# Seven block products in place of eight for a graph network's messages

## The chip, the cores and the metric

The kernel runs on one core of one Trainium2 chip. Its time is the device time of one execution in microseconds; the figure before the change is the median of three runs, 1519.66 us (1519.43 to 1519.81). One further execution was profiled; the hardware profiler gives it a span of 1517.7 us.

## The reference

Four graph layers run one after the other on 64 graphs of 256 nodes with 128 features, all in fp32. Every layer ends in a residual sum and a layer norm, x = layernorm(x + layer(x)). All layers use one weighted adjacency matrix `adj` (256x256). Layer 0 is the one that the change concerns: five steps of a gated recurrent unit whose input is the message `adj @ h`.

```python
def step(h, _):
    m_in = jnp.einsum('nm,bmd->bnd', in_matrix, h)
    m_out = jnp.einsum('nm,bmd->bnd', out_matrix, h)
    av = jnp.concatenate([m_in, m_out], axis=-1)
    u3 = h @ u3_w.T + u3_b
    z = jax.nn.sigmoid(av @ w3_w.T + w3_b + u3)
    r = jax.nn.sigmoid(av @ w4_w.T + w4_b + u3)
    hv = jnp.tanh(av @ w5_w.T + w5_b + (r * h @ u5_w.T + u5_b))
    h = (1.0 - z) * h + z * hv
    return (h, None)
...
x = _layernorm(x + _L0_gnn_ref(x, adj, adj, ...), axis=-1)
```

In and out matrix are the same here, so a step needs one message per graph. Layer 1 mixes two linear maps by a row softmax of edge values (a diagonal part and the rest), layer 2 is an attention layer followed by a graph isomorphism layer, and layer 3 is a polynomial of third order in `adj`.

## The kernel before

Graphs are worked on in pairs, so there are 32 pairs. A pair's state is one tile of 128 partitions by 512 columns. It exists in two layouts. In the layout by tokens, node t*128+p of graph b lies on partition p, in block 2b+t of four blocks of 128 features. In the transposed layout features lie on the partitions and the 512 columns are the nodes of both graphs.

`spread` (L505) forms a message: for either graph two products of 256 columns, the two node blocks of the state being the weights and the two block rows of the transposed adjacency `aT` the moving operand. The result is the transposed message of both graphs in one PSUM bank, and `to_sbuf` copies it to SBUF (`evacuate`, L210 on ACT or L211 on DVE). In terms of 128x128 blocks that is eight products for a message.

A step of layer 0 (`layer0`) then runs in the transposed layout: two products of 512 columns for the gate r (L599, L600), a tanh on ACT (L603), r*h on DVE (L605), one more product into the same bank for the gate z (L607) with a tanh (L609), two products for the candidate (L614, L615) with a tanh (L617), and three DVE operations for the new state (L619, L620, L622). The new state is turned to the layout by tokens for the next message. `turn` does this by a 32x32 block transpose on DVE (L486), one write to DRAM (L488) and four reads from it (L494), all in SP's queue; for the last pairs, as many as `BY_DMA` says for each place, TensorE transposes it instead (L480), with a copy out of PSUM.

The work of 32 pairs is interleaved, and no order is written out by hand. Every piece of work is an `Op` with the values that it reads and writes and one or more ways (an engine, an assumed duration, a function). When the program is built, `Schedule.order` plays the work through: among the operations whose inputs are there and for which a tile is free, it takes the one that can start first, ties going to the one that is latest against a due time (`DUE`, `LAST_DUE`, `LAST`, `HOLD`). The assumed durations are scaled by `MARGIN`, and a consumer on another engine sees a result `LAG` plus `SEEN` later. A way named "DVE+" or "POOL" also takes a common resource "PORT", so the plan doesn't put such operations of the two engines side by side. The instructions of each engine are issued in the order so found, and each waits for the others by semaphores. Buffers are the tiles of `CLASSES`: 34 tiles of class A (512 columns), six of class B (1024), eight PSUM banks (PS), and so on.

Of the kernel before, what the change touches and what calls it, by code (L numbers as in the profile page):

```python
# [9 lines left out]
ALU = mybir.AluOpType  # L10
AX = mybir.AxisListType

P = 128
N = 256
D = 128
STEPS = 5

BY_DMA = {"h": 1, "y": 1, "x1": 2, "x2": 1, "w": 0, "z": 1, "x3": 1}

WARM = 4  # L20

TURN, TT = 0.44, 0.61
# [12 lines left out]

CLASSES = {"X": (512, 15), "T": (512, 3), "A": (512, 34), "H": (520, 4), "B": (1024, 6), "S": (32, 64), "PS": (512, 8), "D": (512, 4), "E": (1024, 8)}

# [4 lines left out]

DUE, LAST_DUE, LAST = 15.0, 7.0, 6

MARGIN, LAG = 1.1, 0.3

HOLD = (0.0, 0.0, 0.0, 110.0)

# [24 lines left out]


class Op:
    def __init__(self, pair, ways, reads, writes, number, dma):
# [5 lines left out]
class Schedule:  # L82
# [6 lines left out]
    def add(self, ways, r=(), w=(), dma=None):  # L89

        op = Op(self.pair, ways, list(r), list(w), len(self.ops), dma)
        for v in op.reads:
            op.before.update(dict.fromkeys(v.writers))
        for v in op.writes:
            op.before.update(dict.fromkeys(v.readers))
        for v in op.reads:
            v.readers.append(op)
        for v in op.writes:  # L100
            v.writers.append(op)
        op.before.pop(op, None)
        op.layer = self.layer
        self.ops.append(op)
        return op
# [5 lines left out]
    def order(self, tiles):  # L111
        for op in self.ops:
            op.waits = len(op.before)
            for b in op.before:
                b.then.append(op)
            for v in dict.fromkeys([*op.reads, *op.writes]):
                v.left += 1
# [7 lines left out]
        while ready:  # L125
            best = None
            for op in ready:
                held = 0.0
                for v in op.writes:
                    if v.cls and v.ap is None:  # L130
                        held = max(held, min((t for t, _ in free[v.cls]), default=1e9))
                if held == 1e9:
                    continue
                for engine, us, fn in op.ways:
                    us = us if engine == "PE" else us * MARGIN
                    start = max(op.ready, held, *(engines[e] for e in USES.get(engine, (engine,))))
                    late = self.due(op.pair) - op.rest + HOLD[op.layer] if op.pair >= 0 else -1e4
                    key = (start + (us if len(op.ways) > 1 else 0.0), late, op.number)
                    if best is None or key < best[0]:
                        best = key, start, op, engine, us, fn  # L140
# [3 lines left out]
            ready.remove(op)  # L144
            for v in op.writes:
                if v.cls and v.ap is None:
                    slot = min(free[v.cls], key=lambda s: s[0])
                    free[v.cls].remove(slot)
                    v.ap = slot[1]
# [6 lines left out]
            out.append((start, op.number, op, fn))  # L156
            for v in dict.fromkeys([*op.reads, *op.writes]):
                v.left -= 1
                v.end = max(v.end, end + op.seen)
                if not v.left and v.cls:  # L160
                    free[v.cls].append((v.end, v.ap))
# [6 lines left out]

            for v in dict.fromkeys([*op.reads, *op.writes]):
                op.__dict__.setdefault("tiles", {})[v] = v.ap  # L170
        assert len(out) == len(self.ops), "operations that wait for one another"
# [5 lines left out]
def kernel(ctx: ExitStack, tc: tile.TileContext, x, xT, adj, adjT, mats, cols, rows, out):  # L177
# [8 lines left out]
    def fixed(shape, name, dtype=F32):  # L186
        return Value(ap=const.tile([P, *shape], dtype, name=name), name=name)
# [190 lines left out]
    for it in range(2):  # L378
# [4 lines left out]
        dve(0.3, lambda it=it, blk=blk: nc.vector.tensor_sub(blk(), blk(), dg.ap[:, it, :]), [lg, dg], [lg])  # L383

    drow, offT = fixed([N], "drow"), fixed([2, N], "offT")

    def diagonal():
        for it in range(2):
            nc.tensor.matmul(t4.at(2, P)[:, it, :], ones.ap[:, :P], dg.ap[:, it, :], start=True, stop=True)
    pe(mm(256), diagonal, [ones, dg], [t4])  # L390
    dve(0.4, lambda: nc.vector.tensor_copy(drow.ap, t4.at(N)), [t4], [drow])
    pe(0.45, lambda: turned(t5.at(2, N), lg.at(2, N)), [lg, ident], [t5])
# [51 lines left out]
    dve(0.25, lambda: nc.vector.tensor_add(vq.ap[:, 1, :], mat("v3"), mat("v6")), [W1], [vq])  # L444

    centre(vx, lambda: vx.ap, 2)
    centre(vq, lambda: vq.ap, 2)
# [51 lines left out]
    def spread(i, right):  # L499

        t = Value("PS", name="ps")
        for b in range(2):
            def fn(b=b):
                for j in range(2):
                    nc.tensor.matmul(t.at(2, N)[:, b, :], tokens(i)[:, 2 * b + j, :], right.ap[:, j, :],  # L505
                                     start=(j == 0), stop=(j == 1))
            pe(mm(512), fn, [i, right], [t])
        return t

    def stats(y, eps=None):  # L510
# [81 lines left out]
    def layer0(x0, hT):  # L592
        h = x0
        for s in range(STEPS):
            mT = to_sbuf(spread(h, aT), "mT")
            t = Value("PS", name="ps")
# [16 lines left out]
            def candidate(t=t, mT=mT, r=r):  # L613
# [4 lines left out]
                [t, bzrh], [hv])  # L618
            dve2(TT, lambda hv=hv, hT=hT: nc.vector.tensor_sub(hv.at(512), hv.at(512), hT.at(512)), [hv, hT], [hv])  # L619
            dve2(TT, lambda hv=hv, z=z: nc.vector.scalar_tensor_tensor(hv.at(512), z.at(512), 1.0, hv.at(512),  # L620
# [5 lines left out]
        y = Value("A", name="y")  # L626
        dve2(TT, lambda: nc.vector.tensor_add(y.at(512), h.at(512), x0.at(512)), [h, x0], [y])
        layer_norm(y, x0)
# [11 lines left out]
    def layer1(x1):  # L640
        qT = to_sbuf(spread(x1, offT), "qT")
        xb, dd = Value("A", name="xb"), lambda: drow.ap[:, None, :].to_broadcast([P, 2, N])
        if by_dma("x1"):
            dT = turn(x1, "dT", "x1")
            dve_or_pool(lambda e: e.tensor_mul(dT.at(2, N), dT.at(2, N), dd()), [drow, dT], [dT])
        else:
            t, dT = transposes(x1), Value("A", name="dT")
            dve(TT, lambda: nc.vector.tensor_mul(dT.at(2, N), t.at(2, N), dd()), [t, drow], [dT])
        dve_or_pool(lambda e: e.tensor_add(tokens(xb), tokens(x1), row("l1_bias", 4)), [x1, rbc], [xb])
# [5 lines left out]
    def layer2(x2):  # L655
# [19 lines left out]

        nm, nm2, den, d2 = (lambda k=k: s.at(32)[:, 4 * k:4 * k + 4] for k in range(4))
        d2v = Value("S", name="d2")
# [5 lines left out]
        def largest():  # L683
            nc.vector.tensor_add(nm(), nm(), hs()[:, :, D])
            nc.vector.tensor_scalar(nm2(), nm(), -1.0, None, op0=ALU.mult)
            nc.vector.scalar_tensor_tensor(nm(), nm(), -0.2, nm2(), op0=ALU.mult, op1=ALU.min)
        dve2(0.5, largest, [s, h], [s])
        for c in range(4):
# [129 lines left out]
```

## Time and profile before

| | before |
|---|---|
| time, median of 3 runs | 1519.66 us |
| profiled span | 1517.7 us |
| TensorE busy | 1509.9 us |
| DVE busy | 1183.2 us |
| ACT busy | 901.1 us |
| Pool busy | 363.0 us |
| messages, `aT` with a state (L505, 1024 records of 256 columns) | mean length 379 ns |
| DMA engines, share of the span in their main queue | 69.5% |

The busy time of an engine is the time in which at least one of its instructions was running. A product in fp32 is two matmul records in the profile, each with its own weight load (PEld). A matmul's recorded length includes the time until its result is out, and the next one starts earlier than that; the distance between starts is what a product costs in a stream. The granted TensorE clock is full in nearly the whole run.

### The profile page before, as it was taken

What the parts mean: (1) busy time and instruction counts of PE and PEld (TensorE: products, weight loads), DVE (VectorE), ACT (ScalarE), POOL (GpSimd) and SP (SyncE); (2) the same over time, 40 slices, a digit from 0 to 9 for tenths busy, and PEclk for the clock granted to TensorE, in tenths of its full rate; (3) what the DMA queues carried; (4) which work ended last, traced back from release to release, by engine and by line L of the source; (5) the groups of instructions that cost most, each with busy time, mean ns of one, the idle gap of its engine ahead of it and who ended that gap; (6) DMA issues with size and microseconds to landing.
All of it is one profiled execution on the core that took longest, in us unless ns stands there. A gap on an engine that the chain in (4) does not pass through costs nothing.

```text
span 1517.7 us, 22720 instructions
## 1 busy us (share of the span) xinstructions
PE 1509.9 (99%) x6300; PEld 1052.0 (69%) x6300; DVE 1183.2 (78%) x2774; ACT 901.1 (59%) x2497; POOL 363.0 (24%) x461
## 2 busy tenths in 40 slices
PE   9999999999999999999999999999999999999998
PEld 6555666666666767777677767666776676779987
DVE  6467878788898889888878778778787877887763
ACT  3444445566667767767556565656565556676752
POOL 0000001122323413332222303112331122224542
PEclk9999999999999999999999999999999999999999
DMA  8354557678688697888868777848777767575552
GB/s 240 71 116 92 121 115 150 139 141 164 147 174 165 141 191 147 171 153 173 168 130 174 153 153 160 160 98 164 140 148 152 148 132 146 102 146 116 122 128 64
DMA packets 949454, 216.79 MB, mean 143 GB/s; under 512 B 728144, under 2 KB 944848, under 8 KB 949328
## 3 DMA queue, kind: packets, MB, share of 16 engines
q1 hardware_dynamic: 949328, 215.34, 69.5%
q8 instruction: 51, 0.84, 0.2%
q14 instruction: 75, 0.61, 0.1%
HBM read 117.12 MB, written 98.11 MB: 142 GB/s over the span
## 4 chain that ended last, share of the span: by engine, by line
PE 99%; SPq 0%; DMA 0%; issue 0%; DVE 0%; POOLq 0%; ACT 0%; ACTq 0%; POOL 0%; DVEq 0%
PE ps L505 29%; PE ps L614 9%; PE ps L607 9%; PE ps L615 9%; PE ps L599 9%; PE ps L600 9%; PE ps L636 8%; PE ps L705 4%; PE ps L751 4%; PE ps L743 4%; PE ps L744 4%; PE ps L664 2%; SPq L494 0%; PE ps L270 0%; PE ps L480 0%; DMA a<-e 0%
## 5 line engine op out<-in xcount | busy, mean ns | idle before, releaser
L210 ACT COPY a<-ps 128x512 f32<-128x512 f32 (+1 forms) x295 | 160.3, 545 | 187.3 <-PE ps L505 129.5
L505 PE MATMUL ps<-aT,a 128*128 128x256 f32 x1024 | 242.7, 379 | 0.3 <-DMA a<-e 0.3
L505 PEld LDWEIGHTS ps<-aT,a 128*128 128x128 f32 x1024 | 193.4, 190 | 69.0 <-issue 46.1
L603 ACT ACTIVATE a<-ps,bzrh 128x512 f32<-128x512 f32 x160 | 109.9, 687 | 166.6 <-PE ps L600 160.2
L617 ACT ACTIVATE a<-ps,bzrh 128x512 f32<-128x512 f32 x160 | 109.8, 686 | 164.2 <-PE ps L615 158.6
L614 PE MATMUL ps<-a,w 128*128 128x512 f32 x320 | 163.5, 592 | 0.0
L600 PE MATMUL ps<-a,w 128*128 128x512 f32 x320 | 163.4, 592 | 0.0
L615 PE MATMUL ps<-a,u5h 128*128 128x512 f32 x320 | 163.4, 592 | 0.0
L607 PE MATMUL ps<-a,w 128*128 128x512 f32 x320 | 162.9, 592 | 0.0
L636 PEld LDWEIGHTS ps<-W,a 128*128 128x128 f32 x1024 | 128.9, 192 | 21.6 <-issue 19.1
L486 DVE STREAM_TRANSPOSE a<-a 128x512 f32<-128x512 f32 x186 | 131.0, 706 | 11.5 <-ACT a L582 4.2
L571 POOL TENSOR_TENSOR s<-s,neg_half 128x4 f32<-128x4 f32 x128 | 137.6, 1075 | 10.1
L605 DVE SCALAR_TENSOR_TENSOR a<-a,a 128x512 f32<-128x512 f32 x128 | 88.3, 690 | 62.6 <-ACT a L603 59.9
L609 ACT ACTIVATE a<-ps,bzrh 128x512 f32<-128x512 f32 x160 | 109.9, 687 | 45.4 <-PE ps L607 43.2
L619 DVE TENSOR_TENSOR a<-a,a 128x512 f32<-128x512 f32 x128 | 90.0, 703 | 54.4 <-ACT a L617 54.3
L636 PE MATMUL ps<-W,a 128*128 128x128 f32 x1024 | 131.3, 275 | 0.0
L599 PE MATMUL ps<-a,W 128*128 128x512 f32 x256 | 130.8, 593 | 0.0
L524 POOL TENSOR_SCALAR s<-s 128x4 f32<-128x4 f32 x64 | 21.5, 336 | 451.9 <-DVE s L521 443.0
L620 DVE SCALAR_TENSOR_TENSOR a<-a,a 128x512 f32<-128x512 f32 x160 | 117.3, 733 | 12.2 <-ACT a L609 7.3
L568 POOL TENSOR_SCALAR s<-s 128x4 f32<-128x4 f32 x96 | 28.5, 297 | 392.0 <-ACT a L563 306.5
L505 PE MATMUL ps<-aT,x 128*128 128x256 f32 x512 | 121.4, 380 | 0.0
L615 PEld LDWEIGHTS ps<-a,u5h 128*128 128x128 f32 x320 | 60.8, 190 | 76.5 <-issue 66.0
(181 smaller groups left out, 2730.3 us busy)
## 6 DMA issues: line engine op xcount, KB each, us to landing
e<-a SPq DMA_DIRECT2D x278, 256.0 KB
a<-e SPq DMA_DIRECT2D x1112, 64.0 KB
e<-b SPq DMA_DIRECT2D x32, 512.0 KB
b<-e SPq DMA_DIRECT2D x128, 128.0 KB
x<-x_in SPq DMA_DIRECT2D x32, 256.0 KB
t<-xT_in SPq DMA_DIRECT2D x32, 256.0 KB
a<-d SPq DMA_DIRECT2D x32, 256.0 KB
y_out<-a SPq DMA_DIRECT2D x32, 256.0 KB
```

The costliest lines, as they stand in the source:

```text
L210: S.add([("ACT", us[0], lambda: nc.scalar.copy(o(), i())), ("DVE", us[1], lambda: nc.vector.tensor_copy(o(), i()))], r, w)
L486: dve(n / 512 * 0.55 + 0.09, lambda: nc.vector.transpose(st.at(n), i.at(n)), [i], [st])
L505: nc.tensor.matmul(t.at(2, N)[:, b, :], tokens(i)[:, 2 * b + j, :], right.ap[:, j, :], start=(j == 0), stop=(j == 1))
L571: pool(1.02, lambda: nc.gpsimd.tensor_tensor(rs(), rs(), neg_half.ap, op=ALU.pow), [s, neg_half], [s])
L599: nc.tensor.matmul(t.at(512), mat("u3"), hT.at(512), start=True, stop=False)
L600: nc.tensor.matmul(t.at(512), w4.ap, mT.at(512), start=False, stop=True)
L603: act(0.59, lambda t=t, r=r: nc.scalar.activation(r.at(512), t.at(512), AF.Tanh, bias=bzrh.ap[:, 1:2], scale=0.5), [t, bzrh], [r])
L607: pe(mm(512), lambda t=t, mT=mT: nc.tensor.matmul(t.at(512), w3.ap, mT.at(512), start=False, stop=True, skip_group_check=True), [w3, mT, t ...
L614: nc.tensor.matmul(t.at(512), w5.ap, mT.at(512), start=True, stop=False)
L615: nc.tensor.matmul(t.at(512), u5h.ap, r.at(512), start=False, stop=True)
L620: dve2(TT, lambda hv=hv, z=z: nc.vector.scalar_tensor_tensor(hv.at(512), z.at(512), 1.0, hv.at(512), op0=ALU.add, op1=ALU.mult), [hv, z], ...
L636: nc.tensor.matmul(tokens(t)[:, c, :], tokens(i)[:, c, :], w(), start=(k == 0), stop=(k == len(lefts) - 1))
```

## The change

For steps 1 to 4 of layer 0 a new helper `spread7` takes the place of `spread` and `to_sbuf`. It treats the state blocks of both graphs and the blocks of `aT` as two 2x2 block matrices and forms their product from seven block products of 128 columns. The recipe needs four sums of state blocks (`add`, in DVE or Pool, chosen by the planner) and four differences of adjacency blocks (`aTt`, formed once). The products go to the four quarters of one PSUM bank, X, Y, Z and V. X, V and Z get two products each and Y one, and X, V and Z are read in between. The first product opens the whole bank. Two copies (`copy`, ACT or DVE) and three sums with a PSUM operand (`plus`, DVE) bring the message together in SBUF. `Part` is a value that stands for a part of a tile, so that the planner orders the parts one by one.

Step 0 of layer 0 and the messages of the other layers keep `spread`. With it come smaller edits. One subtraction of every step of layer 0 (L619) and the residual sum (L627) may go to Pool. Layer 1 scales its input by the diagonal ahead of the turn (on ACT, DVE or Pool), and the diagonal is kept as a column that a DVE reduction makes, no longer as a row that TensorE makes. A small maximum in layer 2 takes two DVE operations for three. The numbers of pairs that are turned by TensorE at the end, the due times, `MARGIN`, `LAG`, `HOLD` and the number of B tiles have new values.

```diff
-BY_DMA = {"h": 1, "y": 1, "x1": 2, "x2": 1, "w": 0, "z": 1, "x3": 1}
+BY_DMA = {"h": 1, "y": 2, "x1": 0, "x2": 1, "w": 3, "z": 3, "x3": 0}
...
+FAST = (1, 2, 3, 4)
...
-DUE, LAST_DUE, LAST = 15.0, 7.0, 6
-MARGIN, LAG = 1.1, 0.3
-HOLD = (0.0, 0.0, 0.0, 110.0)
+DUE, LAST_DUE, LAST = 20.0, 7.0, 12
+MARGIN, LAG = 1.03, 0.8
+HOLD = (0.0, 0.0, -20.0, 110.0)
...
-    def diagonal():
-        for it in range(2):
-            nc.tensor.matmul(t4.at(2, P)[:, it, :], ones.ap[:, :P], dg.ap[:, it, :], start=True, stop=True)
-    pe(mm(256), diagonal, [ones, dg], [t4])
-    dve(0.4, lambda: nc.vector.tensor_copy(drow.ap, t4.at(N)), [t4], [drow])
+    dve(0.3, lambda: nc.vector.tensor_reduce(dcol.ap, dg.ap, AX.X, ALU.add), [dg], [dcol])
...
+    aTt = fixed([4, P], "aTt")
+    blk_a = lambda j, i: aT.ap[:, j, i * P:(i + 1) * P]
+    for k, (p_, q_) in enumerate(((lambda: blk_a(0, 1), lambda: blk_a(0, 0)), (lambda: blk_a(1, 1), lambda: aTt.ap[:, 0, :]),
+                                  (lambda: blk_a(1, 1), lambda: blk_a(0, 1)), (lambda: blk_a(1, 0), lambda: aTt.ap[:, 1, :]))):
+        dve(0.25, lambda k=k, p_=p_, q_=q_: nc.vector.tensor_sub(aTt.ap[:, k, :], p_(), q_()), [aT, aTt], [aTt])
...
+    def spread7(h, right, terms):
...
+        def add(o, x, y, op, r, w):
+            fn = lambda e: e.tensor_tensor(o(), x(), y(), op=op)
+            S.add([("DVE+", 0.2, lambda: fn(nc.vector)), ("POOL", 0.36, lambda: fn(nc.gpsimd))], r, w)
...
+        product(0, H(0, 0), B(0, 0), [h], [X, Y, Z, V], start=True)
+        copy(lambda: blk(o, 3), 0, [X], [o3])
+        add(s1, H(1, 0), H(1, 1), ALU.add, [h], [p1])
+        add(s2, s1, H(0, 0), ALU.subtract, [h, p1], [p2])
+        add(s3, H(0, 0), H(1, 0), ALU.subtract, [h], [p3])
+        add(s4, H(0, 1), s2, ALU.subtract, [h, p2], [p4])
+        product(0, H(0, 1), B(1, 0), [h, X], [X])
+        copy(lambda: blk(o, 0), 0, [X], [o])
+        product(1, s2, T(1), [p2, Y], [Y])
+        plus(lambda: blk(sv, 1), 1, lambda: blk(o, 3), [Y, o3], [p2])
+        product(2, s1, T(0), [p1, V], [V])
+        product(3, s3, T(2), [p3, Z], [Z])
+        plus(lambda: blk(sv, 0), 2, lambda: blk(sv, 1), [V, p2], [p1])
+        product(2, s4, B(1, 1), [p4, V], [V])
+        plus(lambda: blk(o, 3), 3, lambda: blk(sv, 0), [Z, p1, o3], [o])
+        product(3, H(1, 1), T(3), [h, Z], [Z])
+        plus(lambda: o.at(4, P)[:, 1:3, :], 2, lambda: blk(sv, 1)[:, None, :].to_broadcast([P, 2, P]), [V, Z, p2], [o], 2)
+        return o
...
-            mT = to_sbuf(spread(h, aT), "mT")
+            mT = spread7(h, aT, aTt) if s in FAST else to_sbuf(spread(h, aT), "mT")
...
-            dve2(TT, lambda hv=hv, hT=hT: nc.vector.tensor_sub(hv.at(512), hv.at(512), hT.at(512)), [hv, hT], [hv])
+            dve_or_pool(lambda e, hv=hv, hT=hT: e.tensor_sub(hv.at(512), hv.at(512), hT.at(512)), [hv, hT], [hv])
...
-            dve_or_pool(lambda e: e.tensor_mul(dT.at(2, N), dT.at(2, N), dd()), [drow, dT], [dT])
...
+        S.add([("ACT", 1.26, scaled), ("DVE+", TT, lambda: nc.vector.tensor_mul(xd.at(2, 2, D), x1.at(2, 2, D), dc())),
+               ("POOL", 1.27, lambda: nc.gpsimd.tensor_mul(xd.at(2, 2, D), x1.at(2, 2, D), dc()))], [x1, dcol], [xd])
+        dT = turn(xd, "dT", "x1")
...
-            nc.vector.tensor_add(nm(), nm(), hs()[:, :, D])
-            nc.vector.tensor_scalar(nm2(), nm(), -1.0, None, op0=ALU.mult)
-            nc.vector.scalar_tensor_tensor(nm(), nm(), -0.2, nm2(), op0=ALU.mult, op1=ALU.min)
-        dve2(0.5, largest, [s, h], [s])
+            nc.vector.scalar_tensor_tensor(nm(), nm(), -1.0, hs()[:, :, D], op0=ALU.mult, op1=ALU.subtract)
+            nc.vector.scalar_tensor_tensor(nm(), nm(), 0.2, nm(), op0=ALU.mult, op1=ALU.min)
+        dve2(0.25, largest, [s, h], [s])
```

## Prediction

> **What bounds the kernel now.** I began with the page's totals, then the chain that ended last, then who waits for whom on TensorE.
>
> ```profile
> span 1517.7 us, 22720 instructions
> PE 1509.9 (99%) x6300; PEld 1052.0 (69%) x6300; DVE 1183.2 (78%) x2774; ACT 901.1 (59%) x2497; POOL 363.0 (24%) x461
> PE 99%; SPq 0%; DMA 0%; issue 0%; DVE 0%; POOLq 0%; ACT 0%; ACTq 0%; POOL 0%; DVEq 0%
> ```
>
> PE is busy 99% and the chain lies on PE for 99%. A busy PE need not be a full one, so I asked for PE's own waits:
>
> ```profile
> PE ps L270 <- DVE ones L268: 1.2, 1, 1.2
> PE ps L505 <- DMA a<-e: 0.3, 1, 0.3
> ```
>
> After the first 1.2 us PE waits 0.3 us in the whole run. The span is PE's work plus 7.8 us at both ends (1517.7 - 1509.9), so a microsecond of PE work taken away is a microsecond gained as long as PE still never waits. The price of a product comes from start-to-start distances in PE's timeline (columns: start, length, engine, line, count), since lengths overlap:
>
> ```profile
> 704.35 1.95 PE L705 MATMUL ps<-h,b 128*128 128x128 f32 x16
> 706.14 0.60 PE L743 MATMUL ps<-vx,a 128*128 128x256 f32 x2
> ...
> 713.04 1.89 PE L505 MATMUL ps<-aT,a 128*128 128x256 f32 x8
> 713.24 0.69 ACT L603 ACTIVATE a<-ps,bzrh 128x512 f32<-128x512 f32 x1 [2.23 <-PE ps L600]
> ...
> 714.76 1.02 PE L607 MATMUL ps<-a,w 128*128 128x512 f32 x2
> ```
>
> A product is two records. Eight products of 128 columns take 706.14 - 704.35 = 1.79 us, 0.2238 each; four of 256 take 714.76 - 713.04 = 1.72, 0.430 each. Half the columns cost 52%. The ACT row gives the way out of PE: L600's successor starts at 713.04, ACT reads the result at 713.24, 0.20 us later.
>
> DVE is next; where it is fullest it is busy 174.0 of 200 us:
>
> ```profile
> 400.00:600.00 200.00, 199.67 (x842) 135.16 (x841) 174.04 (x388) 140.69 (x400) 62.33 (x69) 1.00 0.83 165
> ```
>
> Two more readings are needed, a 128-column DVE sum and a meeting of DVE and Pool:
>
> ```profile
> 35.21 0.28 DVE L443 TENSOR_TENSOR vq<-W 128x128 f32<-128x128 f32 x1
> 35.42 0.28 DVE L444 TENSOR_TENSOR vq<-W 128x128 f32<-128x128 f32 x1
> ...
> 617.71 1.55 POOL L710 TENSOR_TENSOR a<-a,rbc 128x512 f32<-128x512 f32 x1 [5.66 <-ACT a L582]
> 618.17 1.11 DVE L684 TENSOR_TENSOR s<-s,h 128x4 f32<-128x4 f32 x1
> ```
>
> The sum lasts 0.28 us and gives way after 0.21. L684, four columns wide and 0.165 us at its median, took 1.11 us: it stood until Pool's product was over.
>
> **The Trainium skill.** TensorE: Matmul & The Clock Gate, Part 2, Step-by-step: the drain of one matmul overlaps the fill of the next. The trace agrees: 0.275 us long, 0.112 apart at 128 columns. SBUF - State Buffer, Who interferes with whom: a DVE instruction with two SBUF inputs contends with a GpSimd one that reads SBUF, and the later one blocks; L684 shows it. PSUM - Partial Sum Buffer, PSUM bank collisions: guard PSUM by bank, not by address. No run yet shows the collision, but the changed program's order shows the guard: a product into one quarter of a bank waits for ACT's or DVE's read of another quarter. GPSIMD Engine Reference, 3.1: about 2.6 cycles an element for two inputs. Here 512 columns take 1.28 us (median) and four 0.20, so I estimate 0.47 us for 128.
>
> **The change part by part.** The changed program's order, counted by line, does what the words say: 512 products of 256 columns (steps 1 to 4 of 32 pairs) become 896 of 128; step 0 keeps its own.
>
> PE. Per message 4 x 0.430 = 1.720 becomes 7 x 0.2238 = 1.567; 128 messages save 128 x 0.153 = 19.6 us. Twenty more 128x128 transposes stand in the last pairs (60 for 40; in PE's timeline four of them stand from 1470.61 to 1471.05, so 0.11 each): +2.2. The diagonal's two products go: -0.45. Net -17.9 us.
>
> DVE. Adds in SBUF that the order gives it: 329; sums out of PSUM: 384 of 128 and 128 of 256 columns; 53 small copies. At 0.28, 0.28, 0.415 (L666) and about 0.29 that is 268 us; by start distances (0.20, 0.20, 0.35, 0.20), 198. Off DVE go 119 wide two-input operations (0.69: -82), 32 scalings of L535 (-11), the shortened maximum of layer 2 (-6), six wide copies (-4), and transposes and others (-7): -110. DVE gets to 1271 to 1341 us. Lock waits come on top: the means of the wide rows lie above their medians by some 27 us in all with 70 wide Pool operations; with 168 and 183 small ones I estimate 65 to 80. So some 1310 to 1390 us of about 1500, 87 to 93%.
>
> Pool: 183 x 0.47 + 98 x 1.28 = +211 us, 574 in all. ACT: 203 copies of 128 columns (0.27 from the 256 and 512 rows) for 114 of 512 (0.583), and 124 more row scalings (0.39): about +40. Both stay below 65% and are hidden beside PE, apart from waits below.
>
> The buffers: a message holds one PSUM bank of eight from first product to last read, and an A tile of sums of 34; B gets a seventh tile. The order already has these limits, so their price shows as distances in it. The turn of h through DRAM has more room than before: between the candidate product and the next step's first product stand at least 14.6 us of other PE work (12.3 before, where PE never waited). The x1 scaling before the turn, the moved subtraction and sum, and the new due times sit in stretches with more than 2.6 us of slack, longer than a lock wait (1 us): nothing. SP issues the same 278 + 1112 turns, and 29 + 116 for the attention weights instead of 32 + 128; the queue is off the path before: nothing. The four differences of the adjacency (4 x 0.28) come before DVE's first wait for layer 0 while PE runs step 0: nothing. At the two ends PE is idle for 7.8 us, and 6.3 of it is the chain after the last product (its group ends at 1511.4, the span at 1517.7), which stays; another order there can give or take 1 us, and I count none.
>
> The added wait is the real cost. Within a message PE writes a bank, ACT or DVE reads it, and PE writes it again. A product that waits holds everything behind it on PE. One such exchange takes 0.20 (out of PE) + 0.28 (the sum) + 0.05 (ones written at 1.15, used at 1.20) + 0.19 (weight load) = 0.73 us; 0.55 if the weights are in place. Along the PE order I added up the work that stands between the last product a read needs and the product that waits for that read. Before, the least is 1.7 us. After, 28 places have under 1 us: eight have 0, three 0.22, two 0.43, three 0.45, two 0.67, ten 0.86. At 0.73 they lose 8 x 0.73 + 3 x 0.51 + 2 x 0.30 + 3 x 0.28 + 2 x 0.06 = 8.9 us; at 0.55, 6. Stretches where several reads stand in line add twelve places and 7.6 us (5.4 at the lower price). So 11.3 to 16.5 us of new PE waits, none of it below zero since PE had none to give back. I take 12.5: nearer the lower end, as a wait may not hold up the weights.
>
> Sum: 1517.7 - 17.9 + 12.5 = 1512.3 for the profiled span; the timed runs (1519.43 to 1519.81) stand 2.0 above it, so 1514.
>
> **Rivals.** A, the above: 1514, own range 1510 to 1516.6. For it: PE's own sum is certain. Against: the waits nearly match it.
> B, the exchanges cost little, because other engines are ahead and the weights are loaded early: at most 5 us, 1502 to 1507. For it: PE waited 0.3 us before. Against: places with no work at all between.
> C, the waits reach 16 to 20 us: 1518 to 1522, no change.
> D, slower: the lock between Pool and DVE. DVE runs at 87 to 93%, in its fullest stretches near 98; there it can't catch up a 1 us wait, and a bank's sum comes late to PE. I estimate 70 such waits; if one in five reaches PE that is 14 us on A, 1528. One in thirteen decides (5.4 us more make it 1519.7), one in eight makes it slower by 0.2%. Against: in the program before 174 of 200 busy us on DVE let PE wait 0.3.
> That the change isn't what it says is excluded by the count.
>
> **How the numbers follow.** A measurement tells 0.2%, 3 us, from no change. A 0.48, B 0.12, C 0.15, D 0.25. Faster is A + B, 0.60; same 0.15; slower 0.25. The time is A's, 1514. The range takes in most of B and D: 1503 to 1529. A's and B's own is 1502 to 1516.6.
>
> **What would show it.** PE's work near 1492 us; the 128-column product at 0.224 apart. PE waits of 11 to 17 us, nearly all before products of the new message, released by its sums and copies, 0.5 to 0.75 us each. DVE between 1310 and 1390. B is right if PE waits under 5 us; D if it waits over 24, with DVE rows of over 1 us beside Pool's. I am wrong in the base if 128-column products stand clearly further apart than 0.224.

## The result, and the profile after

The changed kernel takes 1545.24 us (median of 6 runs, 1544.45 to 1549.03), the kernel before beside it 1519.74 us. The ratio is 1.0173, 95% interval 1.0159 to 1.0186: slower, by 25.5 us. I had forecast 1514 us, faster, and a range that ended at 1529.

The page after (span; PE, DVE and the others; the chain by engine):

```profile
span 1542.4 us, 25912 instructions
PE 1507.8 (98%) x7088; PEld 1059.9 (69%) x7088; DVE 1359.0 (88%) x3465; ACT 919.0 (60%) x2725; POOL 598.2 (39%) x742
PE 32%; DVE 6%; DMA 2%; issue 1%; ACT 1%; SPq 1%; POOL 0%; POOLq 0%; ACTq 0%; DVEq 0%
```

The chain no longer lies on PE from end to end. Its shares add up to 43% only, so I read no more from it than that it leaves PE. Who waits for whom on PE, after (us in total, times, longest):

```profile
PE ps L538 <- DVE a L542: 11.9, 21, 2.0
PE ps L538 <- ACT a L545: 2.9, 6, 0.9
PE ps L538 <- DVE a L534: 2.6, 4, 0.8
PE ps L538 <- DVE a L546: 1.8, 5, 0.6
PE ps L670 <- DVE a L542: 1.6, 1, 1.6
```

L538 is a product of the new message, L542 a sum that reads its bank. Before, PE waited 0.3 us in all once it had started. Is a product itself dearer than I thought? PE's timeline, after:

```profile
703.87 0.83 PE L538 MATMUL ps<-aTt,a 128*128 128x128 f32 x6
704.53 0.39 PE L538 MATMUL ps<-aT,a 128*128 128x128 f32 x2
704.76 1.95 PE L692 MATMUL ps<-W,a 128*128 128x128 f32 x16
```

Four products of two records start within 704.76 - 703.87 = 0.89 us, 0.222 each. The price stands, so the time is lost between products. I added, over all neighbours in PE's record, what a start-to-start distance has above the plain one (0.112 us for a record of 128 columns, 0.216 for 256, 0.430 for 512), where that is over 0.04 us. I call this sum PE's gaps: 3.9 us before, 47.0 after. It is more than the waits view shows, because after a wait PE also loses some 0.16 us of overlap between records (one of 128 columns is 0.275 us long, and the next starts 0.112 after it). What is left of the spans is the work: (1542.4 - 47.0) - (1517.7 - 3.9) = -18.4 us. So the change saves what it should, and 43 us of gaps take it back and more.

One stretch and one group of DVE rows point to the reason. First the window from 400 to 600 us, columns as before:

```profile
400.00:600.00 200.00, 193.28 (x907) 133.17 (x908) 184.19 (x465) 121.63 (x359) 71.78 (x89) 1.00 0.72 145
```

DVE went from 174.0 to 184.2 busy us there. Then rows of DVE (busy us, mean ns of one). The first line is the kernel before, whose L620 is L676 after:

```profile
L620 DVE SCALAR_TENSOR_TENSOR a<-a,a 128x512 f32<-128x512 f32 x160 | 117.3, 733 | 12.2 <-ACT a L609 7.3
```

```profile
L676 DVE SCALAR_TENSOR_TENSOR a<-a,a 128x512 f32<-128x512 f32 x160 | 123.3, 774 | 3.7
L534 DVE TENSOR_TENSOR a<-a,a 128x128 f32<-128x128 f32 x194 | 72.8, 379 | 4.8
```

Both read two operands from SBUF. A sum of 128 columns, which lasts 0.285 us while Pool is idle, lasts 0.38 on average. I counted the DVE instructions that last over 0.1 us more than the median of their own row while a two-input operation of 128 columns or more runs on Pool: 46 before, 33 us of extra length in all; 168 after, 101 us. No other DVE instruction is that much longer than its row's median, in either kernel. In what follows these 46 and 168 instructions are called held, and their extra length held time.

### The profile page after: what moved, and what is told of

It reads as the page before. It is cut to its first block, busy times and chain, and to the rows that moved or that the text cites. A ratio compares the mean times of both kernels' runs of the same rounds, so it can differ in the third digit from the quotient of the medians.

```text
span 1542.4 us, 25912 instructions
## 1 busy us (share of the span) xinstructions
PE 1507.8 (98%) x7088; PEld 1059.9 (69%) x7088; DVE 1359.0 (88%) x3465; ACT 919.0 (60%) x2725; POOL 598.2 (39%) x742
## 5 line engine op out<-in xcount | busy, mean ns | idle before, releaser
L542 DVE TENSOR_TENSOR a<-ps,a 128x128 f32<-128x128 f32 (+1 forms) x512 | 156.9, 315 | 63.9 <-PE ps L538 47.0
L538 PEld LDWEIGHTS ps<-aTt,a 128*128 128x128 f32 x1024 | 150.4, 191 | 71.3 <-issue 42.7
L538 PE MATMUL ps<-aTt,a 128*128 128x128 f32 x1024 | 170.4, 277 | 11.8 <-DVE a L542 4.5
L538 PEld LDWEIGHTS ps<-aT,a 128*128 128x128 f32 x768 | 120.4, 191 | 65.2 <-issue 37.7
L496 DVE STREAM_TRANSPOSE a<-a 128x512 f32<-128x512 f32 x215 | 150.8, 704 | 6.9 <-ACT a L704 0.9
L538 PE MATMUL ps<-aT,a 128*128 128x128 f32 x768 | 139.3, 279 | 9.3 <-DVE a L542 7.4
L220 ACT COPY a<-ps 128x512 f32<-128x512 f32 (+1 forms) x173 | 90.0, 523 | 92.4 <-PE ps L515 57.4
L627 POOL TENSOR_TENSOR s<-s,neg_half 128x4 f32<-128x4 f32 x128 | 139.9, 1093 | 10.3
L692 PEld LDWEIGHTS ps<-W,a 128*128 128x128 f32 x1024 | 128.9, 192 | 18.6 <-issue 16.5
L534 POOL TENSOR_TENSOR a<-a 128x128 f32<-128x128 f32 x121 | 66.5, 563 | 188.2 <-DMA a<-e 133.2
L545 ACT COPY a<-ps 128x128 f32<-128x128 f32 x203 | 51.1, 266 | 141.6 <-DVE a L542 71.9
L676 DVE SCALAR_TENSOR_TENSOR a<-a,a 128x512 f32<-128x512 f32 x160 | 123.3, 774 | 3.7
L515 PE MATMUL ps<-aT,x 128*128 128x256 f32 x512 | 123.7, 380 | 1.4 <-DMA x<-x_in 1.4
```

Of the source, the lines that this page charges most:

```text
L496: dve(n / 512 * 0.55 + 0.09, lambda: nc.vector.transpose(st.at(n), i.at(n)), [i], [st])
L538: pe(mm(128), lambda: nc.tensor.matmul(blk(t, k), left(), rt(), start=start, stop=True, skip_group_check=True), [*r, right, terms], w)
L542: dve(0.065 + 0.135 * n, lambda: nc.vector.tensor_add(to(), t.at(4, P)[:, k:k + n, :], other()), r, w)
L627: pool(1.02, lambda: nc.gpsimd.tensor_tensor(rs(), rs(), neg_half.ap, op=ALU.pow), [s, neg_half], [s])
L692: nc.tensor.matmul(tokens(t)[:, c, :], tokens(i)[:, c, :], w(), start=(k == 0), stop=(k == len(lefts) - 1))
```

## Experiments: the numbers of the planner, and eight products

What I expected of these runs speaks of three theories of the new gaps. G: the program guards a PSUM bank as a whole, and the planner doesn't know that. L: DVE reads the bank late because Pool holds up DVE. R: seven products with reads between them need more exchanges of a bank than any order can hide.

**Old numbers.** All edits, with BY_DMA, DUE, LAST, MARGIN, LAG and HOLD of before (one line of the edit is shown).

```
-MARGIN, LAG = 1.03, 0.8
+MARGIN, LAG = 1.1, 0.3
```

> The changed kernel with the planner's numbers of before (turns, due times, margin 1.1, lag 0.3, hold). Theories G and R: a lag of 0.3 leaves less room between a read and the product behind it (by distances in the order 43 places under 1 us after another quarter's read, where the changed kernel has 25), so slower than the changed kernel, 1555 to 1580. Theory L: Pool gets as much work, DVE somewhat less, so 1535 to 1550. A theory that the new numbers are to blame: under 1525.

Measured: 1631.92 us, ratio 1.0735 (1.0719 to 1.0751); gaps 134 us, 59 of them after 1400 us. That is above all the ranges that I gave: with the old numbers the seven products do far worse, so going back to them is no cure.

**Eight products, new numbers.**

```
-FAST = (1, 2, 3, 4)
+FAST = ()
```

> All edits of the change but the seven products: no step uses them, every message keeps eight. Theories G, L and R, which all lay the loss on the new message: 1516 to 1523, PE waits under 4 us. A theory that the new numbers or the smaller edits are to blame: above 1530.

Measured: 1545.68 us, ratio 1.0168 (1.0153 to 1.0184). By the time alone one would blame the other edits and call the seven products a wash. The trace says otherwise: of 27.9 us of gaps 21.6 lie after 1400 us. The stretch from 1500 us to the end at 1544, columns as above:

```profile
1500.00:1546.00 46.00, 22.67 (x85) 17.82 (x83) 12.67 (x48) 6.47 (x17) 7.87 (x11) 0.69 0.12 29
```

PE is busy for 22.7 us of these 44, at a mean clock of 0.69: the last pairs come late and PE runs dry. With these numbers this order ends badly; that is not the changed kernel's illness, which has 1.3 us of gaps after 1400 us.

**Eight products, old numbers.** Both edits together.

> The kernel after with FAST = () and all planner numbers of the kernel before: every other edit of the change stays (diagonal by DVE, scaling before the turn, moved subtraction, 20 more turns on TensorE or fewer, 0.45 us of diagonal less). Theory T (the trace of the run with FAST = () and the new numbers has 21.6 of its 28.0 us of TensorE gaps after 1400 us, so the new numbers, and not the other edits, leave the last pairs late when the messages are of eight products): 1518 to 1525 us. Theory S (the small edits themselves cost the 26 us): 1540 us or more.

Measured: 1527.71 us, ratio 1.005 (1.0033 to 1.0067). That lies between my two ranges: the other edits alone cost 8 us, not 26, and not nothing. Gaps are 12.7 us, 6.6 of them after 1400 us; the longest is a wait of 3.5 us at L801 for a DMA. So the numbers make 18 of the 26 us of the run before, and against this kernel the seven products as they were built lose 17.5 us. I can't say which edit makes the 8.

**The bank as one value.** The planner treats the four quarters as separate values, but the program that comes out guards a bank as a whole. Here the planner knows it.

```
-        X, Y, Z, V = (Part(t) for _ in range(4))
+        X = Y = Z = V = t
```

> The planner treats the four quarters of a message's PSUM bank as one value, so that its order knows that a product waits for the read of any quarter; nothing else differs from the changed kernel. Theory G (the waits come from the guard by bank that the planner doesn't know of): PE's waits fall from 43 us to under 20, time 1515 to 1525. Theory L (the reads are late because DVE stands behind Pool's locks): about the same as the changed kernel, 1538 to 1550. Theory R (seven products with reads in between need more exchanges than any order can hide): PE still waits 35 us or more, now before products that follow a read of their own quarter, 1537 to 1555.

Measured: 1586.58 us, ratio 1.0437 (1.0416 to 1.0457), gaps 90.7 us, 21 of them after 1400 us. That is above the ranges of all three theories. A planner that knows the bank doesn't avoid the waits by that alone: it makes another order, which loses more. Why so much isn't settled.

## Experiments: what Pool holds

In the runs of this section, all but the last, the instructions of PE and DVE stand in the order of the changed kernel, so only durations differ, and what Pool does besides.

**Short Pool operations.** All two-input operations that the planner had given to Pool work on 8 columns of each block in place of all (8 to 32 columns in place of 128 or 512). One of four lines of this kind:

```
-        S.add([("DVE+", TT, lambda: fn(nc.vector)), ("POOL", 1.27, lambda: fn(nc.gpsimd))], r, w)
+        S.add([("DVE+", TT, lambda: fn(nc.vector)), ("POOL", 1.27, lambda: fn(Narrow(nc.gpsimd)))], r, w)
```

> The order of the changed kernel with every two-input operation that it gives to Pool cut to 8 columns of each block (the rest of those sums and products is left out; the A tiles are set to zero at the start), so Pool holds the shared port for a short time only. Theory L: DVE busy falls by 60 us or more and PE's waits from 43 us to under 22, time 1515 to 1525. Theory G: DVE busy falls too, but PE's waits stay above 32 us, 1534 to 1545. Theory R: as G.

Measured: 1529.45 us, ratio 1.0063 (1.0048 to 1.0078). My zeroing of the tiles at the start had put one gap of 8.7 us into it, at 19 us. The same without that:

> As the earlier kernel with short Pool operations, but without zeroing the tiles on Pool at the start (which made one wait of 8.7 us at 19 us there): the first 24 two-input operations on Pool stay whole, every later one works on 8 columns, so work is left out; the order is that of the kernel after. Theory L (Pool's hold of the port makes DVE late, and TensorE waits for DVE): 1529.45 less 8.7, so 1519 to 1523 us. Theory R (the exchanges of seven products with DVE and ACT cost the same whatever Pool does): over 1535 us.

Measured: 1517.43 us, ratio 0.9982 (0.9975 to 0.9989). The loss is gone, and a small gain shows, a little more than theory L had it. But short operations also leave Pool free sooner, and their results come sooner. The next run, the hold-free one, takes the first away: after each cut operation Pool computes a power on 4 columns (or 1), which keeps it busy about as long as the wide one did. A cut operation's own result can still be out before the power is done; but in the changed kernel all waits that end with Pool's wide operations or state sums add up to 2.9 us: 2.2 by TensorE's weight loads, 0.7 by ACT, none by a product.

```
+            f(cut(o), cut(x), cut(y), **k)
+            n = 4 if int(np.prod(o.shape[1:])) >= 256 else 1
+            self.e.tensor_tensor(Narrow.scratch[:, :n], Narrow.one[:, :n], Narrow.half[:, :n], op=ALU.pow)
```

> The order of the kernel after. Each two-input operation of Pool after the first 24 works on 8 columns (work left out) and is followed on Pool by a power on 4 columns (1.09 us by the rows of the profile, and no DVE row is longer beside it) or on 1 column for the sums of 128: Pool is about as long busy as after, but holds nothing of DVE. Theory L (it is the hold of the port that makes DVE late): 1517 to 1524 us, as with short operations. Theory Q (it is that Pool's results come late, whoever holds what): 1535 to 1547 us.

Measured: 1516.59 us, ratio 0.9976 (0.9967 to 0.9985). Its page and its PE waits (L560 and L564 are the lines of L538 and L542):

```profile
span 1515.2 us, 26245 instructions
PE 1498.8 (99%) x7088; PEld 1060.6 (70%) x7088; DVE 1267.7 (84%) x3465; ACT 920.3 (61%) x2725; POOL 634.7 (42%) x1069
```

```profile
PE ps L560 <- DVE a L564: 4.5, 11, 0.8
PE ps L560 <- ACT a L567: 2.0, 5, 0.5
```

Pool is even longer busy than after (634.7 for 598.2 us), and DVE has the same 3465 instructions in 91 us less; held time falls from 101 us to 2. So it is not Pool's load but that a two-input operation of 128 columns or more on Pool holds DVE. The record of PE has the same 7088 matmuls in both, so they can be compared one by one: at 88 places the changed kernel's gap is longer by over 0.04 us, 28.3 us in all; elsewhere shorter by 1.4. That is 26.9 of the 27.2 us between the spans; 20.0 us stand at 62 products of the new message. One of the 88, in the changed kernel:

```profile
985.70 1.27 POOL L675 TENSOR_TENSOR a<-a,a 128x512 f32<-128x512 f32 x1 [4.50 <-ACT a L673]
985.76 1.35 DVE L534 TENSOR_TENSOR a<-a,a 128x128 f32<-128x128 f32 x1
986.92 1.32 POOL L768 TENSOR_TENSOR a<-a,rbc 128x512 f32<-128x512 f32 x1
987.04 1.75 DVE L661 SCALAR_TENSOR_TENSOR a<-a,a 128x512 f32<-128x512 f32 x1
991.53 0.91 DVE L542 TENSOR_TENSOR a<-ps,a 128x128 f32<-128x128 f32 x3
992.49 0.38 PE L538 MATMUL ps<-aT,a 128*128 128x128 f32 x1 [1.96 <-DVE a L542]
```

The same instructions with Pool's cut:

```profile
963.76 0.29 DVE L556 TENSOR_TENSOR a<-a,a 128x128 f32<-128x128 f32 x1
963.97 0.68 DVE L683 SCALAR_TENSOR_TENSOR a<-a,a 128x512 f32<-128x512 f32 x1
967.39 0.90 DVE L564 TENSOR_TENSOR a<-ps,a 128x128 f32<-128x128 f32 x3
968.81 0.61 PE L560 MATMUL ps<-aT,a 128*128 128x128 f32 x4
```

Held, a sum of 0.29 us takes 1.35 and a product of 0.68 takes 1.75, 2.1 us more together. The sum ends 0.14 us after Pool's first operation, the product 0.55 us after the second, most of its own length. DVE takes its queue in order, so the sums that free the bank, behind five more instructions, start at 991.53 - 985.76 = 5.77 us after that sum instead of 967.39 - 963.76 = 3.63. Pool never appears as the releaser of PE; the waits view names DVE, and only DVE's row shows a length that isn't its usual one.

The Trainium skill, SBUF - State Buffer, Who interferes with whom: a DVE instruction with two SBUF inputs contends with a GpSimd one that reads SBUF, one with at most one SBUF input, outside the modes that use both ports, does not. The trace of the changed kernel agrees: of the adds at L534 those that lie for over half their length beside a two-input Pool operation of 512 columns take 1.01 us on average (36 of them), beside one of 128 columns 0.42 (12), those with Pool idle 0.285 (210). The sums of L542 of 128 columns, with one operand in PSUM, take 0.285 us in both cases, and the transposes of L496 0.70. Of the 168 held instructions 167 have two operands in SBUF. (A power on 4 columns is an exception to the section's rule; see the end.)

**Only the wide ones cut.** Operations of 256 and 512 columns are cut, the sums of 128 stay whole.

> The order of the kernel after. Of Pool's two-input operations after the first 24 counted, only those of 512 columns (or 256) are cut to 8 columns (work left out); the state sums of 128 columns stay whole on Pool. Theory W (the holds of 1.3 us by the wide operations, most of which before the change were there too but struck a DVE with nothing urgent, make TensorE wait): 1518 to 1526 us. Theory N (the 183 new sums of 128 columns on Pool do it, by their number): 1535 us or more.

Measured: 1522.41 us, ratio 1.0011 (1.0005 to 1.0018): 22.8 of the 28.7 us that the hold-free run takes off, inside theory W's range. The 183 new short sums on Pool stand for the other 6.

**Only those that the change moved.** Before, the subtraction (L675 after) and the residual sum (L683) were DVE's alone; the change lets Pool take them, and 74 are there.

> The order of the kernel after. Only the wide operations that the change newly lets Pool take (the subtraction of layer 0, 61 of 160, and the residual sum after it, 13 or more) are cut to 8 columns on Pool after the first 8 (work left out); the other wide ones and the short sums stay whole. If the moved ones hold DVE in proportion to their time on Pool (100 of some 230 us of wide operations) : 23 x 0.43 = 10 us off, 1533 to 1538 us. If they do most, being in layer 0 beside the exchanges: 1524 to 1530 us. If they do nothing, as I had counted: 1543 to 1546 us.

Measured: 1529.3 us, ratio 1.0059 (1.0042 to 1.0075): 15.9 us off, so "they do most". The two put back on DVE for real, with other due times, and so in another order (the line of the subtraction is shown):

```
-            dve_or_pool(lambda e, hv=hv, hT=hT: e.tensor_sub(hv.at(512), hv.at(512), hT.at(512)), [hv, hT], [hv])
+            dve2(TT, lambda e=nc.vector, hv=hv, hT=hT: e.tensor_sub(hv.at(512), hv.at(512), hT.at(512)), [hv, hT], [hv])
```

> The subtraction and the residual sum go back to DVE alone (nothing left out), with DUE 25, LAST 10 and HOLD 0, 0, 20, 130 so that the last pairs don't come late in the order. DVE gets 74 x 0.68 = 50 us more work and loses the holds by these. If holds are what counts, wherever the load goes: 1530 to 1540 us. If DVE's load counts as much: 1540 to 1550 us.

Measured: 1528.46 us, ratio 1.0055 (1.004 to 1.007). That is below the lower case that I expected. DVE has this work again, yet its busy time is 1330.2 us for 1359.0, since held time is 56 us for 101. So the run doesn't tell holds from load, and its order differs too; what it gives is a whole kernel that is 16.8 us faster than the changed one with the moved work on DVE.

## Experiments: DVE alone, and two banks

**DVE only.** Nothing wide and no state sum goes to Pool. The line of the state sums:

```
-            S.add([("DVE+", 0.2, lambda: fn(nc.vector)), ("POOL", 0.36, lambda: fn(nc.gpsimd))], r, w)
+            S.add([("DVE+", 0.2, lambda: fn(nc.vector))], r, w)
```

> All two-input operations that the planner could give to Pool are given to DVE alone (or to ACT where that is a way): no hold of the port, nothing left out, planner numbers as after. DVE loses its lengthening (some 95 us by the run with short Pool operations) and takes over Pool's 121 adds of 128 columns at 0.28 us (34 us) and some 60 to 90 operations of 512 columns at 0.7 us (40 to 65 us). Theory L: 1520 to 1530 us, since TensorE waits for late DVE instructions and the load is about the same without holds. Theory that DVE's load as such, wherever it is from, is what makes it late: 1540 to 1550 us, as after.

Measured: 1540.58 us, ratio 1.0135 (1.012 to 1.015). No DVE instruction is held, but DVE is as full as after (1349.5 us), and gaps are 43.6 us, 15.9 of them after 1400 us. That is the range of the theory that load as such counts. With other numbers:

> As the run with DVE only (nothing left out), with planner numbers chosen anew for it: DUE 17, LAST 14, LAG 0.5, HOLD 0, 0, 0, 110. In that run 15.9 of 43.6 us of gaps lay after 1400 us, where the last pairs came late; 22 us lay between 200 and 1400 us. Theory that the tail is a matter of the numbers alone: 1540.6 less 12 to 15, so 1525 to 1529 us. If the smaller LAG lets more exchanges fail: 1530 to 1540 us. Faster than before only if the gaps fall under 18 us.

Measured: 1538.3 us, ratio 1.0118 (1.0101 to 1.0134). The late gaps fall to 0.3 us, but others take their place (42.0 in all), which was the second of my cases. So taking the holds away isn't enough: with one bank and a DVE as full as that, PE's gaps are nearly those of the changed kernel. Whether DVE's load does it or these orders can't be told, since each build has its own.

**Two banks.** The first four products fill a bank before any is read; two go to a second bank; only the seventh is written again.

```
-        product(0, H(0, 1), B(1, 0), [h, X], [X])
...
-        product(3, H(1, 1), T(3), [h, Z], [Z])
+        product(t, 1, s2, T(1), [p2])
+        product(t, 2, s1, T(0), [p1])
+        product(t, 3, s3, T(2), [p3])
+        copy(lambda: blk(o, 3), 0, [t], [o3])
+        product(t2, 0, s4, B(1, 1), [p4], start=True)
+        product(t2, 1, H(1, 1), T(3), [h])
+        product(t, 0, H(0, 1), B(1, 0), [h])
```

> The seven products in two banks: the four first products of a message stand in one bank and are all written before any is read, two more stand in a second bank, and only the seventh (block 0,1 of the state) is written again after one read of 0.27 us by ACT; sums on DVE become 0.28 + 0.41 + 0.28 + 0.41 us per message in place of 0.28 + 0.28 + 0.28 + 0.41, so some 16 us more on DVE in all; one more bank in use per message. Theory R (the handing to and fro between TensorE and the readers of one bank is what costs): TensorE's gaps fall from 47 us to under 20, 1512 to 1522 us. Theory L (late DVE through Pool's holds, wherever TensorE meets it): 1535 to 1550 us, since DVE has no less to do.

Measured: 1568.7 us, ratio 1.0317 (1.0302 to 1.0333). In this kernel a product could stand ahead of the one that opens its bank, so some messages lack products. It is slower than both ranges that I gave: gaps are 71.7 us, 25.9 after 1400 us, and 41 between 200 and 1400, where the changed kernel has 39. Two banks alone didn't help in this order; more can't be read from a kernel that leaves products out. In order, with DVE only and its own numbers:

> DVE only, and the messages in two banks with one rewrite in place of four (the earlier run of two banks let a product go ahead of the one that opens its bank; here they follow in order), and numbers of its own. Nothing left out. Theory R (with the port out of the way, the handing to and fro between TensorE and readers of one bank is what is left, 17 us): gaps between 200 and 1400 us fall from 22 to under 12, total 1510 to 1522 us. Against it: gaps of 20 us or more there, total 1525 to 1545 us, since DVE has 16 us more to do and a message holds two banks.

Measured: 1518.2 us, ratio 0.9982 (0.9974 to 0.999). Nothing is left out, and it is faster than both kernels, by 2.6 us against the kernel before beside it. Its page and its longest PE waits (L537 is the product, L533 the state sum):

```profile
span 1515.6 us, 25544 instructions
PE 1500.3 (99%) x7112; PEld 1062.2 (70%) x7112; DVE 1359.1 (90%) x3692; ACT 973.2 (64%) x2956; POOL 277.2 (18%) x391
```

```profile
PE ps L515 <- DMA x<-x_in: 1.5, 1, 1.5
PE ps L762 <- DMA b<-e: 1.3, 1, 1.3
PE ps L280 <- DVE ones L278: 1.2, 1, 1.2
PE ps L537 <- DVE a L533: 1.1, 3, 0.5
```

DVE is at 90%, as busy as in the changed kernel to 0.1 us, and none of these longest waits of PE is for a reader of the message's bank; gaps are 18.1 us, 11.7 of them between 200 and 1400 us, as theory R had it. The gain over the kernel before is still far below the 18.4 us saved in the change, for 24 more transposes stand on PE (2.7 us) and most gaps are now at other places. Is it the banks or the numbers? The same numbers with one bank, without and with Pool:

> One bank per message as in the change, DVE only, with the planner numbers of the two-bank kernel of 1518.2 us; nothing left out. If the two banks made the difference to the earlier one-bank kernels with DVE only (1540.6 and 1538.3 us): 1533 to 1545 us. If the numbers did: 1515 to 1524 us.

> The kernel after with only the planner numbers of the two-bank kernel of 1518.2 us; Pool takes wide operations as after; nothing left out. If holds and shared bank cost what they cost whatever the numbers are: 1538 to 1560 us (the lag of 0.5 in place of 0.8 gives waits less room). If the numbers made the gain: under 1525 us.

Measured: 1532.55 us, ratio 1.0085 (1.0069 to 1.0102), and 1567.4 us, ratio 1.0308 (1.0293 to 1.0324). The first is 0.45 us below the range for "the two banks made the difference", the second above the range that I gave. The numbers alone don't make the gain: with them, one bank and DVE only is some 6 to 8 us faster than the two such kernels above, and still slower than the kernel before. At equal numbers the build with Pool is 34.8 us slower than the one without (8.3 of it is one wait at L515 for ACT), and one bank is 14.4 us slower than two with DVE only. Each of these pairs differs in its order too. But the place fits: the gaps before products of the new message are 18.5 us with one bank and 3.5 with two. With one bank and DVE only these products still wait for the bank's readers:

```profile
PE ps L538 <- DVE a L542: 4.3, 12, 0.6
PE ps L538 <- ACT a L545: 3.1, 8, 0.5
```

**Two banks, short sums on Pool again.**

> Two banks per message, operations of 512 columns on DVE only, the state sums of 128 columns on DVE or Pool (counted at 0.5 us there), numbers of its own; nothing left out. DVE sheds some 30 us and meets holds of 0.5 us in place of none. If DVE's load is what is left: 1510 to 1516 us. If the short holds cost as much as they shed (5 us in the run in which only wide operations were cut, against 28 for both): 1516 to 1525 us.

Measured: 1519.1 us, ratio 0.9991 (0.9982 to 0.9999). DVE sheds 24 us (1335.3), 107 of its instructions are held by 0.2 us on average, and nothing is gained over the two banks with DVE only. The Trainium skill, PSUM - Partial Sum Buffer, PSUM bank collisions, gives the price of a shared bank its reason, the guard by bank; no run here leaves the guard out.

## Why the prediction was wrong, step by step

The sum, with what was measured: 1517.7 - 18.4 (work of PE) + 16.3 (new gaps without holds, 20.2 - 3.9) + 26.9 (gaps through holds) = 1542.5, against a span of 1542.4. It closes because the terms were taken from the same spans; what it tells is their sizes. Between the 1514 forecast and the 1545 measured, 26.9 us are holds and 3.8 the exchanges.

- *PE, net -17.9.* Right: -18.4 with what changed at the two ends. One reading was off: 64 transposes stand for the 40 of before, not 60, which is 0.45 us.
- *DVE 1310 to 1390, Pool 574, ACT +40.* 1359.0, 598.2 and +17.9. DVE is inside the range, though the held time in it is 101 us where I had 65 to 80; Pool 24 short, ACT too dear, neither of weight for PE.
- *The exchanges, 11.3 to 16.5, taken 12.5.* 16.3 in the hold-free run, whose order is the same: inside the bounds, at the upper one, and 3.8 above what I took. It would have put the time at 1518, which is rival C's; my own upper bound of 16.5 did so too (1518.3), though I let A's range end at 1516.6. And the sum agrees better than its parts: 14.5 us stand before products of the new message, at 60 places of 0.24 us on average, where I had counted 40 at up to 0.73. So distances in PE's order gave the right size, in part by luck.
- *Lock waits, rival D, 14 us at a chance of 0.25.* This is the step that failed. I had the mechanism, the place and the sign that it would show, and counted the waits in DVE's load, but the forecast itself gave PE nothing for them; they cost PE 26.9 us. The rival was also too small. I had some 70 waits and 65 to 80 us of held time in all; there are 168 and 101 us, an increase of 68 on the 33 of before. I took one wait in five to reach PE; the hold-free run takes 99 us of held time away and 26.9 of gaps, so a little over one in four. The argument against D, that before 174 of 200 busy us on DVE let PE wait 0.3, proved nothing: before, by the prediction's own count, at least 1.7 us of PE work stood between the last product that a read needs and the product that waits for the read, so a hold of 1 us could not be seen; after, 28 places have under 1 us. So the change added holds, and it also let those that had been there reach PE, as the runs suggest: the wide operations other than the moved ones, most of them of kinds that Pool had before, make 22.8 - 15.9 = 6.9 us.
- *The moved subtraction in a stretch with over 2.6 us of slack: nothing.* Wrong: with the residual sum that moved too, 15.9 us. I asked whether its own result could be late. The price is not there; it is what stands on DVE while Pool runs it.
- *New due times: nothing.* Neither right nor wrong, since they aren't a term by themselves: eight products with the new numbers lose 18 us against the old ones, seven with the old ones lose 87 us against the new.
- *The turn of h through DRAM has room: nothing.* Right: PE waits once, 0.8 us, at L538 for it.

Not settled: which of the small edits makes the 8 us of eight products with the old numbers, and why the planner that knows the bank does so much worse. How much of the two-bank gain comes from the banks and how much from the order that goes with them can't be told apart either, nor whether DVE's load or the order makes the gaps of the builds with DVE only. What is shown is narrower: in the order of the changed kernel, taking Pool's holds of DVE away, in a run that leaves most of Pool's two-input work out, takes the whole loss away.

## What to carry to other kernels

Before work is moved to Pool, ask which DVE instructions with two SBUF operands will run beside it and who waits behind them in DVE's queue; the moved operation's own slack says nothing on that. Where a producer and its readers share a PSUM bank with little work between, a late reader becomes a wait of TensorE, so count the places with less work between than one late instruction costs, and price holds and exchanges together. An experiment that keeps the order and changes only one duration (columns cut, time filled with something that holds nothing) settles such a question, where one that removes the feature makes the planner find another order.

## What was not expected of the hardware

A power on 4 columns keeps Pool busy for 1.09 us and has two SBUF operands, yet holds no DVE instruction: adds of L534 beside it take 0.286 us, beside Pool operations of 512 columns 1.01. None of the 130 DVE instructions with two SBUF operands of 128 columns or more that lie mostly beside such a power, and beside no wide operation, is over 0.04 us longer than its row's median. So a hold seems to go with the columns read and not with the time that the instruction takes. And a hold isn't small beside what it holds: an add of 128 columns can take 1.40 us, nearly five times its length, for one Pool operation of 512 columns.
